# A four-layer network on one core: a sixth of the weight mixing for two batches as TensorE products, the range count moved behind layer 0, the last product with C on VectorE

## The chip, the core and the metric

The kernel runs on one core of a Trainium2 chip (trn2). A core has five engines, each with a queue of its own that is worked through in order: TensorE (PE, matrix products; its weight loads are listed apart as PEld), VectorE (DVE), ScalarE (ACT), GpSimd (POOL) and SyncE (SP), which here only issues DMAs. They meet through semaphores. Data lies in HBM, in the on-chip SBUF (128 partitions), and in PSUM, eight banks of 128 x 512 floats into which TensorE accumulates. The metric is device microseconds of one execution, as the median of several runs.

## What is computed

Three images of 256 channels, 48 x 48 points, float32, go through four layers. Each adds to x a function of its group norm (32 groups of 8 channels).

```python
x = x + _L0_conv_ref(_gn(x), ...)   # 1x1 convolution, two attention + MLP blocks, 1x1 convolution
x = x + _L1_conv_ref(_gn(x), L1_conv_routing_ws, L1_conv_weight)
x = x + _L2_conv_ref(_gn(x), L2_conv_weight, L2_conv_bias)
x = x + _L3_conv_ref(_gn(x), ...)   # selective scan (Mamba) over the 2304 points
```

Layer 1 mixes eight expert kernels into one 3x3 kernel for each image, and that is what the change bears on most:

```python
pooled = x.mean(axis=(2, 3))
routing = jax.nn.sigmoid(pooled @ routing_ws)
ws = jnp.einsum('ne,eoihw->noihw', routing, weight)
...
return jax.vmap(conv_one)(xp, ws)
```

Layer 2 is one 3x3 convolution with a bias. The core of layer 3 is, for 512 inner channels and 16 states:

```python
def step(hst, inp):
    dt_t, B_t, C_t, u_t = inp
    dA = jnp.exp(dt_t[:, :, None] * A)
    hst = hst * dA + dt_t[:, :, None] * B_t[:, None, :] * u_t[:, :, None]
    y_t = jnp.einsum('bdn,bn->bd', hst, C_t)
    return (hst, y_t)
...
y = ys.transpose(1, 0, 2) + u * D_param
y = y * jax.nn.silu(z)
out = jnp.einsum('bld,cd->blc', y, out_proj_w)
```

Layer 0's softmax is taken without subtracting a row's maximum. The kernel therefore counts whether any of its sums fell out of a safe range (the tile `flag`); if one did, the whole network is run again in an exact form.

## The kernel before

The program is written with a framework that orders each engine's instructions from the data they need and from their place in the text, and gives buffers out in turn. In three stretches the order of the text is kept on PE, DVE, ACT and POOL (`keep_order`): the attention, the end of layer 0, and the scan of layer 3. In the convolutions between them it isn't: there an instruction whose data is ready may be placed ahead. Batches are taken in the order 2, 1, 0.

**Layer 0** lasts to about 1590 us. At the end of its attention the inverse sums lie in a tile; two reductions (L835, L836) and three small operations give a count `ext` for each partition, a product with a column of ones (L841) adds the partitions up, and a copy (L842) writes `flag`. Behind it PE has the second half of the last MLP block (`hidden` L491, `add_back` L502), and ACT has, ahead of its activations, DMA issues for the last 1x1 convolution (L862, L864). Along with that convolution `mixed(2, ...)` already mixes the kernels for batch 2.

**The convolutions, layers 1 and 2.** A unit is one layer and one batch: units 0 to 2 are layer 1, units 3 to 5 layer 2. A unit has two halves (24 rows), a half has two blocks of 128 output channels, and each block is an `output`: six `products` of six PE products each (L1356, weights 128x128, 288 columns; a float32 product has two instructions in the profile), PSUM copies on ACT (`cb`, L1372), and additions on DVE (L1374 to L1386). It is a Winograd form in one direction: `input_transform` makes six images of a half on DVE (L324 to L335), and `kernel_transform` makes from the three columns of the mixed kernel six kernels, by six DVE operations for each half `ct` of the input channels (L256 to L261). A unit's products start when its transformed kernels are there.

Beside units 0 and 1 the kernels of the following batch are mixed (`beside`, `mixed`): 8 experts, 2 halves of input channels, 3 columns, which is 48 pieces of 128 x 768. Each is loaded by SP (L249) into one of six buffers `wconv`. The first expert's are scaled by ACT (L273), the other seven added by DVE, one scalar_tensor_tensor a piece (L275). After each `output` 13 steps of the mixing are written. Beside unit 2 the fixed kernel of layer 2 is loaded and transformed.

After every one of the `products`, `between` takes one step of two further chains: `next_norm`, the group norm for the next use of the batch just done (ACT gives the moments L1400, L1407; PE and DVE the rest, from L184 on, with a power on POOL, L162), and, from unit 4 on, `early_preparation` of layer 3, whose steps wait for those norms. It ends with the gate's projections (`project_z`, L1186) and their copies (`take_z`).

**Layer 3** goes through 18 chunks of 384 points, 8 steps a chunk. A step loads rows of dt (L1505), fills its tile on DVE and POOL (L1535, L1539), has ACT make the decays (L1564) and DVE scan them (L1572), multiplies the states with C on POOL (`times_c`, L1580, 128x3072), sums them on PE (`add_states`, L1597) and gates the sum on DVE (`gate`, L1604). At the very end come, in this order, the sums of the last step, its gate, and for each half `mo` of the channels `project_y` (four products with `out`, L1198, then the residual through a product with the identity, L1202) and `store` (ACT copy L1209, DMA L1210). `bank` are two PSUM banks that layer 3 uses for its small products; in units 0 to 3 they are not in use.

Of the kernel before, what the change touches and what calls it, by code (L numbers as in the profile page):

```python
# [9 lines left out]
F32 = mybir.dt.float32  # L10
I32 = mybir.dt.int32
AF = mybir.ActivationFunctionType
ALU = mybir.AluOpType
# [3 lines left out]
P = 128  # L17
# [3 lines left out]
CT = 2  # L21
# [62 lines left out]
def net(  # L84
# [112 lines left out]
    def at_once(steps):  # L197

        try:
            while True:  # L200
                next(steps)
        except StopIteration as end:
            return end.value
# [56 lines left out]
        nc.vector.tensor_tensor(u[:, 3, :, ct, :], t, g1, ALU.subtract)  # L260
        nc.vector.tensor_tensor(g1, t, g1, ALU.add)  # L261

    def mixed(b, pool):

        u = weights[b] = pool.tile([P, 6, 3, CT, 256], F32, name="u")
        for e in range(EXPERTS):
            for ct in range(CT):
                for dx in range(3):
                    wt = part_of_kernel(we[e], ct, dx)
                    re = route[b][:, e : e + 1]  # L270
                    dst = u[:, dx, :, ct, :]
                    if e == 0:
                        nc.scalar.activation(dst, wt, AF.Copy, scale=re)  # L273
                    else:
                        nc.vector.scalar_tensor_tensor(dst, wt, re, dst, ALU.mult, ALU.add)  # L275
                    yield
        for ct in range(CT):
            kernel_transform(u, ct)
            yield

    def plain(pool):
        u = weights[B] = pool.tile([P, 6, 3, CT, 256], F32, name="u")
        for ct in range(CT):
            for dx in range(3):
                nc.sync.dma_start(
                    u[:, dx, :, ct, :],
                    w2[ct * P : (ct + 1) * P, dx * 768 : (dx + 1) * 768].rearrange(
                        "p (y o) -> p y o", y=3
                    ),
                )  # L290
                yield
            kernel_transform(u, ct)
            yield
# [66 lines left out]
    with ExitStack() as l0:  # L360
# [95 lines left out]
        def one():  # L456
            return psm.tile([P, 512], F32, tag="m", name="ps_m")
# [50 lines left out]
        with ExitStack() as p2:  # L508
# [323 lines left out]
            if not exact:  # L832

                ext = small.tile([P, 2], F32, name="ext")
                nc.vector.tensor_reduce(ext[:, 0:1], sums, AX.X, ALU.max)  # L835
                nc.vector.tensor_reduce(ext[:, 1:2], sums, AX.X, ALU.min)  # L836
                nc.vector.tensor_scalar(ext[:, 0:1], ext[:, 0:1], 1.0 / SUM_MIN, None, ALU.is_gt)
                nc.vector.tensor_scalar(ext[:, 1:2], ext[:, 1:2], 1.0 / SUM_MAX, None, ALU.is_lt)
                nc.vector.tensor_tensor(ext[:, 0:1], ext[:, 0:1], ext[:, 1:2], ALU.add)
                pe = one()  # L840
                nc.tensor.matmul(pe[:1, :1], ext[:, 0:1], ones[:, 0:1], start=True, stop=True)  # L841
                nc.vector.tensor_copy(flag, pe[:1, :1])  # L842

        early.close()
        psums.close()
# [92 lines left out]
        keep_order(tc, listed, mark)  # L938
        for steps in small_steps:
            at_once(steps)  # L940

# [105 lines left out]
    def in_order(t):  # L1049

        return t.rearrange("p (j n) -> p n j", j=4)
# [141 lines left out]
            k.sz = room(k, "sz")  # L1193
        nc.scalar.copy(k.sz[:, m, :], bank[j])

    def project_y(k, mo):
        for m in range(DI):
            nc.tensor.matmul(  # L1198
                bank[mo], w("out", m * 256 + mo * P, P), k.sz[:, m, :],
                start=m == 0, stop=False,  # L1200
            )
        nc.tensor.matmul(bank[mo], ident, in_order(k.ot[:, mo, :]), start=False, stop=True)  # L1202

    def residual(k):
        k.ot = room(k, "ot")
# [140 lines left out]
    with ExitStack() as l1:  # L1346
# [40 lines left out]


        units = [(layer, b) for layer in range(2) for b in ORDER]
        beside = {0: mixed(1, upools[1]), 1: mixed(0, upools[0]), 2: plain(upools[1])}  # L1390
        halves = [(k, h) for k in range(len(units)) for h in range(2)]

        def moments(b):
# [19 lines left out]
        def next_norm(layer, b):  # L1413

            last = layer and b == ORDER[-1]
            known = None if last else moments(b)
            for _ in range(5):
                yield
            _, sc, sh = yield from group_norm_steps(b, pss, "s", known=known)
            if layer == 0:  # L1420
                norms[b] = sixth(sc, sh)
            else:
                keep = const.tile([P, 2, CT], F32, name=f"norm3{b}")
                nc.vector.tensor_copy(keep[:, 0, :], sc)
                nc.vector.tensor_copy(keep[:, 1, :], sh)
                norm3[b] = keep[:, 0, :], keep[:, 1, :]
# [53 lines left out]
    with ExitStack() as l3:  # L1480
# [95 lines left out]
        def times_c(s):  # L1576
            at, m, h = steps[s]
            cb = chunks[at].bc[1][:, 2 * h : 2 * h + 2, :].unsqueeze(2)
            hc = scn.tile([P, 2, 4, CH], F32, name="hc")
            nc.gpsimd.tensor_tensor(  # L1580
                hc, tiles[s][:, :, :, 1:], cb.broadcast_to([P, 2, 4, CH]), ALU.mult
            )
            tiles[s] = hc
# [18 lines left out]
        def gate(at, m):  # L1602
            k = chunks[at]
            nc.vector.tensor_tensor(k.sz[:, m, :], k.y_ps[:, :CH], k.sz[:, m, :], ALU.mult)  # L1604
# [10 lines left out]
        for s, (at, m, h) in enumerate(steps):  # L1615
            if m == 0 and h == 1 and at + 2 <= last:
                fetch(at + 2)
            for part in range(8):
                j = 4 * m + 2 * h + part // 4
                scan(s, part)  # L1620
                decay(8 * s + part + 3)
                if part == 4 and s + 1 < len(steps):
                    first_states(s + 1)
                if part % 4 == 1:
                    if h == 1 and part == 5 and s >= 3:
                        gate(*steps[s - 3][:2])
                    run(at, j, MID)
                if part % 4 == 3:
                    run(at, j, LATE)
                if part == 3:  # L1630
                    run(at, j, PE_)
                    if s + 1 < len(steps) and h == 0:
                        more = [(at, m + 1)] if m + 1 < DI else [(at + 1, 0)]
                        for c, n in more:
                            if c <= last:
                                rows = getattr(chunks[c], "rows", {})
                                chunks[c].rows = {**rows, n: spread(chunks[c], n)}
            if s + 1 < len(steps):
                fill(s + 1)
            last_states(s)  # L1640
            times_c(s)
            run(at, 4 * m + 2 * h + 1, PE_)
            if s >= 1:
                add_states(s - 1)

            if h == 0 and s + 2 < len(steps):
                spread_pe(chunks[steps[s + 2][0]], steps[s + 2][1])
        end = len(steps) - 1
        add_states(end)
        gate(*steps[end][:2])  # L1650
        k = chunks[last]
        residual(k)
        for mo in range(2):
            project_y(k, mo)
            store(k, mo)
        keep_order(tc, listed, mark)
    late_pools.close()
# [112 lines left out]
```

## Time and profile before

| | |
|---|---|
| median of 3 runs | 3594.66 us (3594.13 to 3596.95) |
| profiled execution | 3598.05 us, its span 3596.3 us |
| mean granted TensorE clock | 0.934 |
| PE busy | 3179.0 us (88%) |
| DVE busy | 3003.0 us (84%) |
| ACT busy | 2333.6 us (65%) |
| POOL busy | 1440.4 us (40%) |

All times in the profile are of that one execution and run from the start of its span. A row of a timeline has its start, its length, the engine, the line of the kernel, the operation, what it writes and reads, a count, and in brackets how long the engine stood idle before it and what ended that. Rows of the same kind in close succession are merged. "SPq" and "ACTq" are the issue of DMAs. A row of stretches has, for one piece of the span, the busy time of each engine. Ends of matrix products are modelled.

### The profile page before, as it was taken

The numbers are of one execution on the slowest core, as the hardware profiler recorded it, in microseconds if no ns is written. First come the engines' busy times: TensorE is split into PE (matmuls) and PEld (weight loads), VectorE is DVE, ScalarE is ACT, GpSimd is POOL, SyncE is SP. The second block draws the span as 40 slices with busy tenths as digits, with TensorE's granted clock in tenths as the row PEclk, the third lists the DMA queues.
The fourth block names the chain that finished last, engine by engine and source line by source line (L and its number), as shares of the span: only waits on it lengthen the run. The fifth ranks groups of instructions, "written<-read, shape, count | busy, mean of one in ns | idle before, by whom it ended". The sixth has DMA issues, their size and how long they took to land. (4 is left out here: it accounts for less than half of the span.)

```text
span 3596.3 us, 45582 instructions
## 1 busy us (share of the span) xinstructions
PE 3179.0 (88%) x17154; PEld 1438.0 (40%) x17154; DVE 3003.0 (84%) x3304; ACT 2333.6 (65%) x3477; POOL 1440.4 (40%) x386
## 2 busy tenths in 40 slices
PE   7999999999999999977899987888888888788875
PEld 4323232352322324546677743333333333333331
DVE  4798989959989896479965379999999999999996
ACT  2788787748877875332123447777777777777774
POOL 0000000000000000210000059999999999999998
PEclk9999999999999999988999988889999999888986
DMA  4000000000000001756402234444444444444441
GB/s 181 3 1 1 1 2 1 1 40 1 1 1 1 2 1 60 243 171 219 164 28 58 60 75 116 102 112 106 111 98 111 102 108 101 118 106 107 107 106 36
DMA packets 170648, 266.50 MB, mean 74 GB/s; under 512 B 42849, under 2 KB 137633, under 8 KB 168498
## 3 DMA queue, kind: packets, MB, share of 16 engines
q1 hardware_dynamic: 152082, 243.44, 25.2%
q10 hardware_dynamic: 18336, 20.06, 1.7%
q8 instruction: 136, 2.23, 0.3%
q14 instruction: 94, 0.77, 0.1%
HBM read 216.31 MB, written 46.89 MB: 73 GB/s over the span
## 5 line engine op out<-in xcount | busy, mean ns | idle before, releaser
L610 ACT ACTIVATE pt<-ps_s 128x1024 f32<-128x1024 f32 x972 | 939.0, 1022 | 236.9 <-PE ps_s L606 219.3
L1572 DVE TENSOR_TENSOR_SCAN hs<-ps_da,hs 128x385 f32<-128x385 f32 x1152 | 1012.8, 939 | 63.2 <-ACT ps_da L1564 45.4
L686 DVE TENSOR_TENSOR part<-part,pt 128x2048 f32<-128x2048 f32 x396 | 906.5, 2289 | 79.4 <-ACT pt L610 54.8
L1564 ACT ACTIVATE ps_da<-dtr,u 128x384 f32<-128x384 f32 x1152 | 658.0, 582 | 311.1 <-DVE hs L1572 292.6
L162 POOL TENSOR_TENSOR rstd<-ve,mhalf 128x2 f32<-128x2 f32 (+1 forms) x26 | 17.9, 691 | 1529.1 <-DVE ve L160 1529.1
L606 PE MATMUL ps_s<-q,kt 32*128 32x512 f32 (+1 forms) x4320 | 615.2, 593 | 2.3 <-DVE q L567 0.9
L619 PE MATMUL acc<-pt,vt 128*32 128x512 f32 (+1 forms) x4320 | 522.3, 562 | 8.1 <-DVE o L666 8.0
L1356 PE MATMUL ps_c<-vt,u 128*128 128x288 f32 x1728 | 430.0, 410 | 45.7 <-DVE u L261 45.7
L1580 POOL TENSOR_TENSOR hc<-hs,x 128x3072 f32<-128x3072 f32 x72 | 445.6, 6188 | 37.8 <-PE ps_g L1155 13.4
L1580 POOL TENSOR_TENSOR hc<-hs,bc 128x3072 f32<-128x3072 f32 x72 | 444.1, 6169 | 37.7 <-DVE hs L1572 14.1
L1109 PE MATMUL ps_g<-u 128*128 128x384 f32 x1152 | 389.2, 493 | 3.1 <-ACT u L1118 3.1
L1356 PEld LDWEIGHTS ps_c<-vt,u 128*128 128x128 f32 x1728 | 330.3, 192 | 140.1 <-issue 34.8
L606 PEld LDWEIGHTS ps_s<-q,kt 32*128 32x128 f32 x4320 | 220.0, 183 | 388.5 <-issue 227.1
L1109 PEld LDWEIGHTS ps_g<-u 128*128 128x128 f32 x1152 | 215.0, 190 | 174.5 <-issue 14.0
L1597 PE MATMUL ps_y<-hc,u 128*32 128x384 f32 x2304 | 246.1, 550 | 30.7 <-POOL hc L1580 27.4
L1539 POOL TENSOR_TENSOR hs<-dtur,x 128x1536 f32<-128x1536 f32 x72 | 247.9, 3443 | 17.4 <-DMA dtur<-dtud 8.8
L1539 POOL TENSOR_TENSOR hs<-dtur,bc 128x1536 f32<-128x1536 f32 x72 | 248.5, 3451 | 6.5 <-ACT ps_g L1087 2.4
L619 PEld LDWEIGHTS acc<-pt,vt 128*32 128x32 f32 x4320 | 95.7, 108 | 363.8 <-issue 328.1
L1155 PE MATMUL ps_g<-wconv,u 17*128 17x384 f32 x144 | 79.2, 684 | 97.2 <-ACT x L1176 97.2
L1372 ACT COPY cb<-ps_c 128x288 f32<-128x288 f32 x48 | 19.0, 396 | 219.1 <-PE ps_c L1356 200.7
L1067 PE MATMUL ps_g<-wconv,u 128*128 128x384 f32 x144 | 87.5, 780 | 67.0 <-ACT x L1176 66.6
L1597 PEld LDWEIGHTS ps_y<-hc,u 128*32 128x32 f32 x2304 | 64.6, 118 | 201.9 <-issue 151.0
(236 smaller groups left out, 3517.1 us busy)
## 6 DMA issues: line engine op xcount, KB each, us to landing
wconv<-in_we SPq DMA_DIRECT2D x144, 384.0 KB, 4.3
dtr<-dtd SPq DMA_DIRECT2D x288, 192.0 KB, 3.8
dtur<-dtud SPq DMA_DIRECT2D x288, 96.0 KB, 4.1
wconv<-xd SPq DMA_DIRECT2D x36, 384.0 KB, 4.4
x<-bcd SPq DMA_DIRECT2D x72, 192.0 KB, 5.8
dtd<-x SPq DMA_DIRECT2D x36, 384.0 KB, 2.4
bc<-bcd SPq DMA_DIRECT2D x72, 192.0 KB, 5.5
yc<-ycat ACTq DMA_DIRECT2D x18, 576.0 KB, 4.7
```

Of the source, the lines that this page charges most:

```text
L606: nc.tensor.matmul(s[:, j, cols], kt[r, mt * P : (mt + 1) * P], q[r, :n], start=True, stop=True,)
L610: nc.scalar.activation(p[:, h0 : h0 + 2, :], s, AF.Exp)
L619: nc.tensor.matmul(acc[h * HD : (h + 1) * HD, :n], vt[:, mt, g * P + h * HD : g * P + (h + 1) * HD], p[:, h, cols], start=mt == 0, stop=mt ...
L686: nc.vector.tensor_tensor(part, first_p if group == 1 else part, p, ALU.add)
L1067: nc.tensor.matmul(bank[to], w3v["less"][:, int(to != ct), :], k.xg[:, ct, :], start=ct == 0, stop=ct == CT - 1,)
L1109: nc.tensor.matmul(bank[m % 2], w3v["wtap"][:, tap, ct, m * P : (m + 1) * P], k.xn[:, ct, tap : tap + CH], start=tap == 0 and ct == 0, sto ...
L1356: nc.tensor.matmul(pc[:, :HN], u[:, i, dy, ct, m * P : (m + 1) * P], vt[:, i, ct, dy * TW : dy * TW + HN], start=ct == 0 and dy == 0, stop ...
L1539: nc.gpsimd.tensor_tensor(hs[:, :, 2:4, 1:], k.rows[m][1].unsqueeze(1).broadcast_to([P, 2, 2, CH]), bb, ALU.mult,)
L1564: nc.scalar.activation(slots[n % 3][:, 1 : CH + 1], chunks[at].rows[m][0][:, q, :], AF.Exp, scale=amat[:, col : col + 1],)
L1572: nc.vector.tensor_tensor_scan(b, slots[(8 * s + part) % 3][:, : CH + 1], b, 0.0, ALU.mult, ALU.add)
L1580: nc.gpsimd.tensor_tensor(hc, tiles[s][:, :, :, 1:], cb.broadcast_to([P, 2, 4, CH]), ALU.mult)
L1597: nc.tensor.matmul(k.y_ps[32 * q : 32 * q + 32, :CH], fold, hc[:, g, q, :], start=False, stop=h == 1 and g == 1,)
```

## The change

Four edits:

1. `mixed` for batches 1 and 0 (`shared`): for the second half of input channels (`ct` 1) and the third column (`dx` 2), which are 8 of the 48 pieces, the mixing is done by TensorE. For each expert ACT scales the identity by the routing weight, and two products of 384 columns accumulate in the two banks `bank`; after the last expert four ACT copies bring the sum to SBUF.
2. `next_norm` waits nine steps instead of five ahead of its first TensorE product.
3. The product and the copy that end the range count stand behind the end of layer 0.
4. In the last step of layer 3 the product with C is two DVE operations of 128x1536; and of the last chunk's projection the identity product (now first) and three of the four products with `out`, for both halves, come ahead of the sums of the last step. The load of the residual moves with them.

```diff
-    def mixed(b, pool):
+    def mixed(b, pool, shared=False):
...
-                    if e == 0:
+                    if shared and ct == CT - 1 and dx == 2:
+                        flat = wt.rearrange("p y o -> p (y o)")
+                        each = tmp.tile([P, P], F32, name="each")
+                        nc.scalar.activation(each, ident, AF.Copy, scale=re)
+                        for j in range(2):
+                            nc.tensor.matmul(
+                                bank[j], each, flat[:, j * 384 : (j + 1) * 384],
+                                start=e == 0, stop=e == EXPERTS - 1,
+                            )
+                        if e == EXPERTS - 1:
+                            for y, o, n in ((0, 0, 256), (1, 0, 128), (1, 128, 128), (2, 0, 256)):
+                                at = y * 256 + o
+                                j = at // 384
+                                nc.scalar.copy(
+                                    dst[:, y, o : o + n], bank[j][:, at - 384 * j : at - 384 * j + n]
+                                )
+                    elif e == 0:
                         nc.scalar.activation(dst, wt, AF.Copy, scale=re)
                     else:
                         nc.vector.scalar_tensor_tensor(dst, wt, re, dst, ALU.mult, ALU.add)
...
-                pe = one()
-                nc.tensor.matmul(pe[:1, :1], ext[:, 0:1], ones[:, 0:1], start=True, stop=True)
-                nc.vector.tensor_copy(flag, pe[:1, :1])
...
         for steps in small_steps:
             at_once(steps)
+        if not exact:
+            pe = one()
+            nc.tensor.matmul(pe[:1, :1], ext[:, 0:1], ones[:, 0:1], start=True, stop=True)
+            nc.vector.tensor_copy(flag, pe[:1, :1])
...
-    def project_y(k, mo):
-        for m in range(DI):
+    def project_y(k, mo, lo=0, hi=DI):
+        if lo == 0:
+            nc.tensor.matmul(bank[mo], ident, in_order(k.ot[:, mo, :]), start=True, stop=False)
+        for m in range(lo, hi):
             nc.tensor.matmul(
                 bank[mo], w("out", m * 256 + mo * P, P), k.sz[:, m, :],
-                start=m == 0, stop=False,
+                start=False, stop=m == DI - 1,
             )
-        nc.tensor.matmul(bank[mo], ident, in_order(k.ot[:, mo, :]), start=False, stop=True)
...
-        beside = {0: mixed(1, upools[1]), 1: mixed(0, upools[0]), 2: plain(upools[1])}
+        beside = {0: mixed(1, upools[1], True), 1: mixed(0, upools[0], True), 2: plain(upools[1])}
...
-            for _ in range(5):
+            for _ in range(9):
                 yield
...
+            if s == len(steps) - 1:
+                for g in range(2):
+                    nc.vector.tensor_tensor(
+                        hc[:, g], tiles[s][:, g, :, 1:],
+                        cb[:, g].broadcast_to([P, 4, CH]), ALU.mult,
+                    )
+                tiles[s] = hc
+                return
...
         end = len(steps) - 1
-        add_states(end)
-        gate(*steps[end][:2])
         k = chunks[last]
         residual(k)
         for mo in range(2):
-            project_y(k, mo)
+            project_y(k, mo, 0, DI - 1)
+        add_states(end)
+        gate(*steps[end][:2])
+        for mo in range(2):
+            project_y(k, mo, DI - 1, DI)
             store(k, mo)
```

Since `project_y` is one function for all chunks, the identity product comes first in every chunk.

## The prediction

> **What bounds the kernel now.** I read three views: busy time in equal stretches, to find where which engine is full; the timeline around each edit; the chain of waits at the end. The page's averages (PE 88%, DVE 84%) mix stages. The stretches cut at the PE's own stops in units 0 to 2 of the convolutions read (us, then busy PE, PEld, DVE, ACT, POOL, granted clock, DMA share, GB/s):
>
> ```profile
> 1592.30:1665.70 73.40, 73.26 (x296) 56.67 (x296) 72.22 (x128) 13.59 (x19) 1.55 (x4) 0.97 0.63 215
> 1665.70:1685.30 19.60, 0.58 (x2) 0.51 (x3) 19.60 (x27) 13.01 (x13) 0.69 (x3) 0.56 0.70 240
> 1685.30:1757.30 72.00, 71.92 (x290) 55.93 (x290) 71.24 (x124) 10.39 (x15) 2.10 (x4) 0.98 0.59 203
> 1757.30:1774.30 17.00, 0.58 (x2) 0.50 (x2) 17.00 (x21) 7.40 (x7) 0.69 (x3) 0.59 0.63 209
> 1774.30:2098.00 323.70, 323.15 (x1286) 242.99 (x1286) 181.84 (x392) 93.89 (x125) 7.92 (x23) 1.00 0.16 42
> ```
>
> VectorE (DVE) is full in all four first rows, so DVE sets when unit 2 starts (1774.3). TensorE stands idle for 19.6 and 17.0 us in them. From 1774.3 to 2098.0 it is the reverse: PE is full, DVE half full. A gain in units 0 and 1 thus moves the start of a stretch that PE then fills without a hole, and passes on whole. The timeline names what PE waits for:
>
> ```profile
> 1668.09 8.44 DVE L275 SCALAR_TENSOR_TENSOR u<-wconv,route,u 128x768 f32<-128x768 f32 x9
> 1685.32 22.23 PE L1356 MATMUL ps_c<-vt,u 128*128 128x288 f32 x84 [14.20 <-DVE u L261]
> 1774.34 22.11 PE L1356 MATMUL ps_c<-vt,u 128*128 128x288 f32 x84 [12.29 <-DVE u L261]
> ```
>
> The mixing (L275) and then the kernel transform (L256 to L261) must end on DVE before the next unit's first product. The end of the kernel is one chain: last product with C on POOL, PE, ACT, store.
>
> **Part 1, the mixing of batches 1 and 0.** Removed from DVE: 7 instructions a batch, 14 in all. Nine in a row take 8.44 us, so 0.94 each: 13.1 us, all on DVE's full stretch; call it 13.0. Removed from ACT: one of 0.93 us a batch. Added a batch: 8 ScalarE scalings of the 128x128 identity, a form not in the trace, between 0.20 (L1404, one column) and 0.39 us (L1372, 288 columns); I take 0.28. Four PSUM copies of 128 or 256 columns, at most 0.39 each (L1372). ACT gains about 2.7 us a unit where it is busy 13.6 of 73.4: hidden. On PE: 16 products a batch, 32 instructions, since every f32 product has two here. Those of 128x384 run 32 in 10 us at full clock around 1440 (0.3125 each): 10.0 us a batch, 20.0 us in all. No DMA is added; the same 48 weight pieces are loaded.
>
> Does PE hold that? From 1592.3 to 1774.3 are 182.0 us, of which PE is busy 73.3+0.6+71.9+0.6 = 146.4. Free: 35.6; minus 20.0 added, minus the 13.0 by which the stretch shrinks: 2.6 us left. PE and DVE come out level, so stalls of one now cost. Two are new. (a) PE's queue is in order: a product waiting for its weight piece holds all convolution products behind it, and DVE waits for those. DVE waited for such pieces only 0.4 us over 98 instructions, ACT 12.9 us over 12 (the first expert). (b) At a unit's end, last piece, ACT scaling (0.28), four PE instructions (1.25) and ACT copies (up to 1.3) stand before the transform of that half: 2.8 us, against 0.94 for the DVE instruction in its place. The other half's transform (6 x 0.87 = 5.2 us) can cover this if it goes first; in the trace the halves alternate. I charge 3 us for both together; bounds 0 and, for stalls, the rivals below. Unit 2 starts 13.0 - 3.0 = **10.0 us earlier**.
>
> **The restart.** The 84 instructions after 1774.34 take 22.1 us, against 19.5 at the steady 0.2326 (43 in 10 us): 2.6 us lost after 12 us of idleness. Taking this row as it is, the loss stays. The Trainium skill, "TensorE: Matmul & The Clock Gate", Part 1, says that the array drops to half clock only after an idle window of some 3.4 us. By my sum PE ends unit 1 about when the weights are ready, so under the rule 2.6 us more go, by the row 0. I take the rule, **-2.6**, as the trace has this loss only behind long gaps.
>
> **Part 2, the norm four products later** (range 5 to 9). What units 0 to 2 give is used three units later. On PE it moves the small L184, which twice waited for ACT's moments (4.9, 4.2 us), into a place where these are done: that is why PE can use its free time; no separate gain; POOL's power L162, which moves along, finds POOL idle. In units 4 and 5 everything behind the norms in the early preparation of layer 3 moves by four products. The trace follows program order there:
>
> ```profile
> 2084.76 1.45 PE L1186 MATMUL ps_g<-u 128*128 128x384 f32 x4
> 2086.05 11.80 PE L1356 MATMUL ps_c<-vt,u 128*128 128x288 f32 x48
> 2097.93 1.82 SPq L1505 DMA_DIRECT2D dtr<-dtd  x4
> ```
>
> 48 instructions are four products: after the change the last two gate projections (L1186, eight instructions x 0.32 = 2.6 us) come behind the last product. The first load of layer 3 goes out 0.1 us after that product, so it goes up to 2.6 us earlier. The first fill on DVE (ends 2104.6; first scan 2107.6) and the PE work before it don't. Bounds -2.6 and 0; I take **-1.5**. Nothing new queues on SP.
>
> **Part 3, the flag count.** PE waited 6.2 us for it, yet little was held:
>
> ```profile
> 1408.92 1.28 ACT L496 ACT_TABLE_LOAD   x1 [6.43 <-DMA yc<-ycat]
> 1410.21 2.00 ACT L496 ACTIVATE f<-ps_s,fb 128x384 f32<-128x384 f32 x4
> 1410.98 0.19 PE L841 MATMUL ps_m<-ones,ext 128*1 128x1 f32 x2 [6.15 <-DVE ext L839]
> 1411.10 0.50 PEld L502 LDWEIGHTS acc<-f,w0b 128*128 128x128 f32 x2
> ```
>
> L502 behind it needs ACT's first activation, done at 1410.7. The wait that takes its place ends 0.35 us earlier. The moved copy costs 0.15 on DVE, in its full stretch at worst. **-0.2**; bounds -0.4 and +0.2.
>
> **Part 4, the tail.**
>
> ```profile
> 3566.86 12.27 POOL L1580 TENSOR_TENSOR hc<-hs,bc 128x3072 f32<-128x3072 f32 x2
> 3569.13 1.80 DVE L1572 TENSOR_TENSOR_SCAN hs<-ps_da,hs 128x385 f32<-128x385 f32 x2
> 3573.08 2.79 PE L1597 MATMUL ps_y<-hc,u 128*32 128x384 f32 x16 [2.16 <-POOL hc L1580]
> 3590.35 0.48 ACT L1209 COPY wconv<-ps_g 128x384 f32<-128x384 f32 x1 [3.41 <-PE ps_g L1202]
> ```
>
> The scans end at 3570.9; POOL ends its last product at 3579.1. On DVE it is two halves of 1536, nearest L1535 (1.73, one operand in PSUM): ready at 3574.4. Against this stands "SBUF — State Buffer", section "SBUF: two separate sides": a DVE instruction with two SBUF inputs and a GpSimd one that reads SBUF exclude each other, the later waits. POOL's next-to-last runs to 3573.0, so by the rule the product is ready at 3576.5. The trace has the reverse case: POOL's L883 takes 2.14 instead of 1.80 us where it starts 0.4 us before a DVE L275 ends. I take the rule; it costs nothing, as PE is later. PE, in order: next-to-last sums to 3575.9; projection ahead, 4 identity instructions x 0.655 (L1202) and 12 x 0.32 (L1198 at full clock) = 6.5, and 0.5 while the clock rises: 3582.9; last sums at full clock 1.5: 3584.4; gate 0.6; two instructions 0.7; ACT 0.48; the second half 0.6 behind: 3586.9, where before it ended at 3590.8. The stores now follow closely, so I give back 0.2: **-3.7**. All at half clock it would be +2; -4.5 at best. The residual's load, moved up too, costs nothing: the last L1206 went out at 3465.5, 120 us early, and SP's queue has nothing behind it until the stores. In the other 17 chunks the identity product moves ahead of four products; its load (3.7 us to landing) is written three half-steps, some 13 us, ahead: 0.
>
> **Sum**: -10.0 - 2.6 - 1.5 - 0.2 - 3.7 = -18.0 us. The profiled execution took 3598.05 (span 3596.30); the median, 3594.66, lies 3.4 below. The difference carries over: **3576.7, say 3577 us**.
>
> **Rivals.** *PE becomes the bound of the mixing units.* For: only 2.6 us are left, 16 pairs of new products, each in order behind a load. At 1 us of stall a pair: 16 us, less the 2.6 left and 2.6 of restart in the first unit: 10.8 of the 13.0 are gone, the later restart gain too. -2.2 - 1.5 - 0.2 - 3.7 = -7.6: 3587. Against: DVE's 0.4 us.
> *The weight pieces hold PE (slower).* A load takes 4.3 us to landing and its buffer is one of six, freed in SP's order by DVE, which may itself wait for products behind the held pair. At half a landing, 2.15 x 16 = 34.4, less 5.2: 29.2 against 13.0: +16.2 - 5.4 = +10.8: 3605. From (13.0 + 5.2)/16 = 1.15 us a pair on the mixing loses; from 1.95 on the kernel is over 0.2% slower.
> *The mixing does nothing*, the order on DVE breaking up so that the freed time is idle: -5.4, 3589. Against: DVE had other ready work through both units.
>
> **Chances.** Forecast 0.66 (3570 to 3586), PE bound 0.16, no gain of the mixing 0.08, slower 0.10. A measurement here tells 0.2% (7.2 us) from none. Faster: 0.65 + 0.11 of PE bound and 0.01 = 0.77; same 0.12; slower 0.11. Best ends together (-13 - 2.6 - 2.6 - 0.4 - 4.5) are -23.1, 3571.6; low 3570. High 3592 takes in both middle rivals.
>
> **What would show it.** L275 14 fewer; unit 2 starting near 1764 with a gap before it under 4 us and its first 84 instructions near 20 us; no PE waits on weight pieces over 1 us; L1186's last eight behind the last product; the last ACT copy some 4 us nearer to the last scan. Wrong it is if DVE shows idle stretches in units 0 and 1, or PE waits for pieces at each expert.

## The result, and the profile after

The changed kernel takes 3581.61 us (median of 4 runs, 3580.52 to 3583.59), the kernel before 3594.39 us in the same rounds (4 runs, 3592.78 to 3596.95): a ratio of 0.9964, 95% interval 0.9947 to 0.9982. The medians differ by 12.8 us, the two profiled spans by 14.4 (3596.3 and 3581.9). The forecast was 18.0 less; 3581.6 lies in its range of 3570 to 3592. Faster it is, but two of the five terms were clearly off, and they are the matter of what follows.

Busy time in stretches, cut at the first product of units 1 and 2 (columns as in the prediction: us, busy PE, PEld, DVE, ACT, POOL, granted clock, DMA share, GB/s), changed kernel:

```profile
1590.90:1677.77 86.87, 85.01 (x333) 63.43 (x333) 82.20 (x144) 17.89 (x30) 1.53 (x4) 0.97 0.63 215
1677.77:1766.19 88.42, 83.23 (x324) 62.12 (x324) 83.65 (x139) 28.21 (x43) 2.08 (x7) 0.97 0.65 220
1766.19:2090.00 323.81, 323.68 (x1290) 244.17 (x1292) 186.51 (x404) 94.58 (x126) 7.71 (x26) 0.99 0.17 45
```

The first two rows are units 0 and 1. TensorE (PE) is no longer idle for 19.6 and 17.0 us at a unit's end; it is busy for 85.0 of 86.9 and 83.2 of 88.4 us. VectorE (DVE), which was full before (1.2 and 0.8 us idle), now is idle for 4.7 and 4.8 us of them. Both engines are at 94 to 98%: they came out level, as the prediction's sum had it. In the third row PE is full as before.

Time went as follows, before and after, from the timelines. *Unit 0 to unit 2*: 182.0 and 175.3 us, 6.7 less. *Unit 2's start to the last convolution record's start*: 323.1 and 320.6, 2.5 less. *Last scan's end to the span's end*: 25.4 and 22.1, 3.3 less. Unit 0 started 1.4 us earlier, and some 0.5 us lie in the rest. (A record is one instruction of the profile.)

The waits of DVE in units 0 and 1, for the mixing line (L294, the old L275), and those of SP's queue, first the kernel before, then the changed one (us in all, times, longest):

```profile
SPq L249 <- DVE u L275: 99.3, 72, 14.3
```

```profile
SPq L249 <- DVE u L294: 68.2, 56, 10.9
...
SPq L249 <- PE ps_g L280: 18.4, 6, 8.8
```

Before, a load of a weight piece (L249) only ever stood for DVE to free a buffer of the ring, which hurts nobody as DVE was the slow one. Now it stands six times, 18.4 us, for PE's mixing product. The group line of the mixing shows what that does:

```profile
L294 DVE SCALAR_TENSOR_TENSOR u<-wconv,route,u 128x768 f32<-128x768 f32 x112 | 108.2, 1010 | 7.0 <-DMA wconv<-in_we 7.0
```

There are 112 instructions where there were 126, the 14 fewer that were counted; and DVE idled 7.0 us for pieces, where it was 0.4. The largest such wait, in the timeline of unit 1:

```profile
1717.52 2.74 PE L280 MATMUL ps_g<-wconv,each 128*128 128x384 f32 x8
...
1720.10 17.62 PE L1377 MATMUL ps_c<-vt,u 128*128 128x288 f32 x72
...
1737.56 1.45 PE L280 MATMUL ps_g<-wconv,each 128*128 128x384 f32 x4
...
1742.51 1.56 PE L280 MATMUL ps_g<-wconv,each 128*128 128x384 f32 x4 [1.07 <-DMA wconv<-in_we]
...
1745.07 1.02 DVE L294 SCALAR_TENSOR_TENSOR u<-wconv,route,u 128x768 f32<-128x768 f32 x1 [2.72 <-DMA wconv<-in_we]
```

PE takes the pieces of two experts (8 records of L280), then 72 convolution records for 17.6 us, then the next two. A piece that lands early stays in its buffer, one of six, for as long. The second of the pair at 1742.51 had not landed, and DVE's next piece, behind it on SP's queue, came 2.72 us late.

The end of the convolutions, changed kernel, answers to the lines on L1186 before (now L1206):

```profile
2081.24 5.98 PE L1377 MATMUL ps_c<-vt,u 128*128 128x288 f32 x24
2087.05 2.75 PE L1206 MATMUL ps_g<-u 128*128 128x384 f32 x8
2087.30 1.81 SPq L1526 DMA_DIRECT2D dtr<-dtd  x4
```

The last eight gate instructions stand behind the last product, and layer 3's first load goes out 0.1 us after that product's end. The flag's place:

```profile
1409.98 2.00 ACT L515 ACTIVATE f<-ps_s,fb 128x384 f32<-128x384 f32 x4
...
1410.62 1.65 PE L521 MATMUL acc<-f,w0b 128*128 128x384 f32 x2 [6.01 <-ACT f L515]
```

PE now waits 6.01 us for ScalarE's first activation, where it had waited 6.15 for the flag. And the tail, first PE's last sums in the kernel before, which stood 3.32 us for POOL's product, then the changed kernel:

```profile
3579.19 2.45 PE L1597 MATMUL ps_y<-hc,u 128*32 128x384 f32 x16 [3.32 <-POOLq L1691]
```

```profile
3555.28 6.14 POOL L1610 TENSOR_TENSOR hc<-hs,bc 128x3072 f32<-128x3072 f32 x1
...
3559.68 5.04 DVE L1604 TENSOR_TENSOR hc<-hs,bc 128x1536 f32<-128x1536 f32 x2
3561.48 2.79 PE L1627 MATMUL ps_y<-hc,u 128*32 128x384 f32 x16 [1.73 <-POOLq L1724]
...
3569.04 2.11 PE L1220 MATMUL ps_g<-sz,u 128*128 128x384 f32 x6
3571.09 1.50 PE L1627 MATMUL ps_y<-hc,u 128*32 128x384 f32 x16
...
3574.86 0.48 ACT L1230 COPY wconv<-ps_g 128x384 f32<-128x384 f32 x1 [0.17 <-PE ps_g L1220]
```

The last product with C is ready at 3564.72; PE comes to it only at 3571.09, behind the projection ahead. The last copy ends 15.6 us behind the last scan (3559.76), before 19.9.

### The profile page after: what moved, and what is told of

Same layout as the page of the kernel before. It is cut to its first block, busy times and chain, and to the rows that moved or that the text cites. A ratio compares the mean times of both kernels' runs of the same rounds, so it can differ in the third digit from the quotient of the medians.

```text
span 3581.9 us, 45734 instructions
## 1 busy us (share of the span) xinstructions
PE 3197.7 (89%) x17218; PEld 1451.1 (41%) x17218; DVE 2995.9 (84%) x3292; ACT 2337.2 (65%) x3499; POOL 1432.3 (40%) x385
## 5 line engine op out<-in xcount | busy, mean ns | idle before, releaser
L1610 POOL TENSOR_TENSOR hc<-hs,bc 128x3072 f32<-128x3072 f32 x71 | 437.9, 6168 | 36.7 <-PE ps_g L1175 13.6
L1377 PE MATMUL ps_c<-vt,u 128*128 128x288 f32 x1728 | 432.8, 411 | 20.5 <-DVE u L261 20.5
```

The lines of the kernel that those rows point to most:

```text
L1377: nc.tensor.matmul(pc[:, :HN], u[:, i, dy, ct, m * P : (m + 1) * P], vt[:, i, ct, dy * TW : dy * TW + HN], start=ct == 0 and dy == 0, stop ...
L1610: nc.gpsimd.tensor_tensor(hc, tiles[s][:, :, :, 1:], cb.broadcast_to([P, 2, 4, CH]), ALU.mult)
```

## The experiments

Single profiles of one kernel differ in two places that have nothing to do with the edits. Unit 0's first product lay between 1585.6 and 1592.3 us in all the profiles; in the stage before it PE's waits for the load `yc` came to 2.0 us in mix_one, where unit 0 starts first, and to 6.4 in spread, where it is among the last; and layer 3, from first to last scan, took 1459.6 to 1463.3 us. So each experiment is read by the lengths of the stages between, not by its total.

| kernel | unit 0 starts | units 0+1 | DVE's piece waits | unit 2 to last record | last scan to end |
|---|---|---|---|---|---|
| before | 1592.3 | 182.0 | 0.4 | 323.1 | 25.4 |
| changed | 1590.9 | 175.3 | 7.0 | 320.6 | 22.1 |
| after_again | 1589.6 | 175.2 | 6.8 | 320.7 | 22.1 |
| undo_mix | 1587.4 | 183.6 | 1.9 | 320.2 | 22.1 |
| mix_one | 1585.6 | 180.5 | 4.2 | 320.4 | 22.0 |
| own | 1586.2 | 175.3 | 7.2 | 318.9 | 24.0 |
| spread | 1592.1 | 174.8 | 5.6 | 321.7 | 22.0 |
| spread_all | (1588.9) | 171.9 | 0.5 | 320.1 | 22.1 |
| warm | 1590.1 | 173.8 | 6.5 | 319.7 | 22.2 |
| norm5 | 1590.9 | 174.6 | 5.9 | 323.8 | 22.1 |
| tail_pool | 1587.6 | 175.4 | 6.6 | 320.2 | 22.2 |
| tail_late | 1588.8 | 174.4 | 5.9 | 320.2 | 21.0 |
| best | 1589.7 | 173.1 | 4.4 | 320.2 | 20.7 |
| best_warm | 1590.1 | 172.6 | 2.7 | 320.8 | 21.0 |

(spread_all: from when unit 0 could have started, 1.10 us after the start of its last transform instruction, the distance in the others; it started at 1591.7.)

**The mixing taken back, for both batches and for one.**

```diff
-beside = {0: mixed(1, upools[1], True), 1: mixed(0, upools[0], True), 2: plain(upools[1])}
+beside = {0: mixed(1, upools[1]), 1: mixed(0, upools[0]), 2: plain(upools[1])}        # undo_mix
+beside = {0: mixed(1, upools[1], True), 1: mixed(0, upools[0]), 2: plain(upools[1])}  # mix_one
```

> The changed kernel with the shared mixing taken back for both batches; the other three parts stay. Changed kernel: 86.87 us from unit 0's first product to unit 1's, 88.42 from unit 1's to unit 2's, together 175.3, span 3581.9. Theory (the mixing alone made these two stages shorter): together 182.0 +- 0.5 as before the change, span near 3588.6. Rival (the later norm frees part of it, since its small product no longer stops PE inside the units): together 180 or less.

> Only batch 1's mixing (beside unit 0) is shared with TensorE; batch 0's (beside unit 1) is all on VectorE as before. Theory (in unit 1 the waits for weight pieces eat the gain): unit 0 to 1 near 86.9, unit 1 to 2 near 89.0, so the span only 0.5 to 1 us over the changed kernel's, and VectorE waits for pieces in unit 1 fall from 4.1 to under 1 us. Rival (each of the two gives half, and unit 1 only looks short because work slid over the border): unit 1 to 2 near 91 to 92, span 3 us over.

undo_mix gave 93.8 and 89.7 us, 183.6 in all: 1.1 over the theory's upper end, nowhere near the rival's 180. The later norm frees nothing in these two units; all of the 6.7 to 8.3 us is the mixing's. (Of the 1.6 us by which undo_mix is longer than the kernel before, DVE's waits for pieces, 1.9 in place of 0.4, make up nearly all; why they came isn't shown.) mix_one went against its theory: unit 0 took 86.6 us, but unit 1, with all of its mixing on DVE, 93.9 and not 89.0. The rival fits (91 to 92 was even short). Read unit by unit the changed kernel seemed to gain 6.1 us in unit 0 and 0.6 in unit 1; in truth work slid over the border (DVE was busy 83.65 us in unit 1 and not the 81.8 that 88.26 less seven instructions would be). Sharing batch 0 is worth 180.5 - 175.3 = 5.2 us, sharing batch 1 the other 1.5 to 3.1. (Its span, 3581.3, is no longer than the changed kernel's only because unit 0 happened to start 5.3 us earlier.)

**A buffer of its own for half of PE's pieces; the pieces spread evenly; both.**

```diff
-wt = part_of_kernel(we[e], ct, dx)
+if shared and ct == CT - 1 and dx == 2 and e % 2 == 0:        # own
+    wt = tmp.tile([P, 3 * 256], F32, name="wpe", bufs=1)
+    nc.sync.dma_start(wt, we[e][ct * P : (ct + 1) * P, dx * 768 : (dx + 1) * 768])
+    wt = wt.rearrange("p (y o) -> p y o", y=3)
+else:
+    wt = part_of_kernel(we[e], ct, dx)
...
-add = tmp.tile([P, HN], F32, name=f"add{i}")
+add = tmp.tile([P, HN], F32, name=f"add{i}", bufs=1)          # sub{i} too
```

```diff
 def between():                                                # spread
     next(pending, None)
+    for _ in range(2):
+        next(beside.get(at_unit, iter(())), None)
...
-                for _ in range(13):
+                for _ in range(1):
                     next(beside.get(k, iter(())), None)
```

> TensorE's pieces of experts 0, 2, 4, 6 get a buffer of their own beside the six of the ring (the room comes from giving VectorE's sums and differences, which only it writes and reads, one buffer in place of two). Hold theory (a piece sits in the ring until PE comes to it through 72 convolution records, and the loads behind it on SP's queue wait): VectorE's waits for pieces fall from 7.0 to under 3 us and the two stages from 175.3 to 171 to 173. Rival (PE and VectorE, both nearly full and in order, set the length; a wait that goes comes back at the next product): waits fall, stages stay at 174.5 or more.

> The mixing's steps are issued two behind each convolution product and one behind each output, not thirteen behind each output; so PE's products with the pieces stand every 36 convolution records, not two together every 72. Ring of six as in the changed kernel. Hold theory: each piece is held half as long, waits of VectorE for pieces under 3 us, stages together 171 to 173. Rival (PE/VectorE order): 174.5 or more, as the even spread only moves the waits, or PE now waits over 3 us for pieces.

Both missed what the hold theory wanted. own's waits stayed at 7.2 us and its stages at 175.3, to a tenth those of the changed kernel. Its SP queue shows why it was no clean test:

```profile
SPq L274 <- PE ps_g L287: 19.6, 2, 10.7
...
SPq L249 <- PE ps_g L287: 4.2, 3, 2.1
```

L274 is the load into the new buffer. It stood 19.6 us for PE to use the piece before, with all other loads behind it: the hold had moved, 23.8 us in place of 18.4. spread gave 174.8 us with 5.6 of waits, within the scatter of 174.4 to 175.4 over the four profiles that have the changed kernel's convolutions (changed, after_again, tail_pool, tail_late). Alone, neither helps. Whether both together do was the next run: the even spread, and all of PE's pieces in the one buffer of their own (the condition on e left out).

> Mixing steps issued two behind each convolution product (as in the run spread), and all of TensorE's pieces in one buffer of their own, so that the six of the ring serve VectorE alone. Units 0 and 1 together took 175.3 (changed kernel), 175.3 (own) and 174.8 us (spread), VectorE's waits for pieces 7.0, 7.2 and 5.6. Hold theory: only now is the ring free of held pieces; waits under 2 us and the two units in 169 to 172. Rival (in-order PE and VectorE set it): 174.5 or more whatever the waits. Second rival (one buffer makes SP's queue wait for each piece): waits over 8 us, units over 177.

The first theory held: 0.5 us of waits, 171.9 us in the two units. In unit 1, whose start needs no such correction:

```profile
1676.50:1760.82 84.32, 81.91 (x320) 61.67 (x320) 81.35 (x136) 21.56 (x32) 2.78 (x7) 0.97 0.59 198
```

84.3 us in place of 88.4, with DVE's waits for pieces there 0.3 in place of 4.1 us. Yet the queue of SP did not stop standing for PE in this run, and PE stood ahead of unit 0:

```profile
SPq L274 <- PE ps_g L287: 31.3, 9, 12.5
...
1588.98 2.90 PE L287 MATMUL ps_g<-wpe,each 128*128 128x384 f32 x4 [3.41 <-DMA wpe<-in_we]
```

That fits a cost not of the standing queue as such, but of the ring behind it running empty: with none of PE's pieces in it, six buffers serve DVE's five pieces of an expert. Which of the two edits carries more of it can't be said, as each alone gave nothing. The price is at the other end: PE stood 13.6 us in all for pieces, 13.2 of them ahead of unit 0 for batch 1's first ones, loaded one after the other, and unit 0's first product came 2.7 us late.

Two things more differ in this run. Twelve of PE's 64 mixing records stood ahead of unit 0, and unit 0 began at full clock (granted 1.00 from 1592 to 1594 us, where the changed kernel had 0.50), so PE had more room; this run can't tell their part from that of the waits. The run best, below, has neither. And not all of the gain arrived: the waits for pieces fell by 6.5 us, the two units by 3.4, as DVE then waited more for others, such as 2.3 us in unit 0 for PE's small norm product (L184).

**The restart.** Four products of no use follow the last expert's mixing product:

```diff
 if e == EXPERTS - 1:
+    warm = pss.tile([P, 512], F32, tag="s", name="ps_warm")
+    for j in range(4):
+        nc.tensor.matmul(warm[:, :384], each, xs[0 if b else 2][:, 0, :384],
+                         start=True, stop=True)
```

> The changed kernel with four products of no use on TensorE (128x384, into a free bank) behind the last expert's mixing product of both shared batches, so that the array has work in the gap before units 1 and 2. Theory (the restart at half clock is the array's idleness alone): granted clock 1.0 through both starts, the first 72 convolution records of unit 1 in about 16.8 us in place of 19.4, the first 69 of unit 2 in about 16.1 in place of 19.1; from unit 2's start to the end some 3 us less than the changed kernel's 1815.7. Rival (the slow start is not the clock but operands or queue): records stay slow, nothing gained.

The clock did as the theory had it. The starts of units 1 and 2 in the changed kernel, as rows of the timeline:

```profile
1677.77 19.42 PE L1377 MATMUL ps_c<-vt,u 128*128 128x288 f32 x72 [0.15 <-DVE u L261]
...
1766.19 23.99 PE L1377 MATMUL ps_c<-vt,u 128*128 128x288 f32 x89 [2.85 <-DVE u L261]
```

Stretches of PE around them (us, busy PE, granted clock, DMA share, GB/s), the changed kernel and then warm:

```profile
1677.77:1682.00 4.23, 4.23 (x11) 0.60 0.50 157
...
1766.19:1771.00 4.81, 4.80 (x11) 0.55 0.33 113
```

```profile
1676.66:1682.00 5.34, 3.84 (x15) 1.00 0.30 88
...
1763.92:1770.00 6.08, 5.50 (x23) 1.00 0.63 211
```

The time followed only in part. In warm PE is busy only 3.84 of 5.34 us at unit 1's start: it runs into the transform of the second half, which DVE has yet to do, and waits 1.50 us (in unit 2 0.73). Unit 1's first 72 records end 19.5 us after its start (19.4 in the changed kernel). The 16.8 us expected were too few in any case: at full clock 72 records take 17.62 us and 48 take 11.80 (rows in this text), so one takes 5.82 / 24 = 0.2425 us and not 0.2326. By that rate the restarts of the changed kernel cost PE 19.42 - 17.62 = 1.8 us in unit 1 and 23.99 - 21.7 = 2.2 in unit 2, not 3 each. From unit 2's start to the last record 319.7 us stand against 320.2 to 320.7 of the four profiles with the changed kernel's convolutions, so 0.4 to 1.0 us less, not 3; units 0 and 1 became 0.6 to 1.6 us shorter. That is 1.0 to 2.4 of the 4.0 us; the rest lies beside work that DVE has yet to do. Even the part behind unit 2's start is not clear of scatter: four kernels ran that start at full clock (own, spread_all, warm, best_warm), and the stretch took them 318.9 to 320.8 us.

**The norm alone.**

```diff
-            for _ in range(9):
+            for _ in range(5):
```

> The changed kernel with the norm back five products into the next unit in place of nine; the rest stays. Changed kernel, two profiles: units 0 and 1 together 175.3 and 175.2 us, from unit 2's start to the last convolution record 320.6 and 320.7. Theory (the later norm is worth 2.5 us at layer 3's preparation and, now that TensorE is nearly full in units 0 and 1, also frees it there of the wait for ScalarE's moments): 323.1 and 177 or more. Rival (only the preparation of layer 3 gains): 323.1 and 175.2 +- 0.6. Second rival (the 2.5 us come from something else): 320.7.

The first rival: from unit 2 to the last record 323.8 us (3.1 more), units 0 and 1 174.6 (no worse). The lines of norm5 show the gate projections between the products again, with 48 records behind them:

```profile
2075.36 2.75 PE L1206 MATMUL ps_g<-u 128*128 128x384 f32 x8
2077.94 11.80 PE L1377 MATMUL ps_c<-vt,u 128*128 128x288 f32 x48
2089.82 1.82 SPq L1526 DMA_DIRECT2D dtr<-dtd  x4
```

**The tail, one edit at a time.**

```diff
-            if s == len(steps) - 1:                           # tail_pool
+            if s == len(steps):
```

```diff
-        for mo in range(2):                                   # tail_late
-            project_y(k, mo, 0, DI - 1)
         add_states(end)
         gate(*steps[end][:2])
         for mo in range(2):
-            project_y(k, mo, DI - 1, DI)
+            project_y(k, mo)
             store(k, mo)
```

> The changed kernel with the last product with C back on POOL; the projection stays ahead of it. From the last scan's end to the end of the span the kernel before took 25.4 us, the changed one 22.1. Theory (the two edits of the tail replace each other: POOL's product would be ready near 6.1 us after its next-to-last, 3.6 us before PE has done the projection ahead): 22.1 +- 0.4. Rival (the product's engine made the gain): about 25.

> The changed kernel with the whole last projection behind the last product again; that product stays on VectorE. Theory (the two edits replace each other: PE never waits for VectorE's product, so the order of its own work is indifferent): 22.1 +- 0.4 from the last scan's end. Rival (the projection ahead made the gain): about 25.

The theory held for tail_pool to 0.1 us (22.2) and was exceeded by tail_late (21.0). Lines of tail_pool, then of tail_late:

```profile
3549.40 12.30 POOL L1610 TENSOR_TENSOR hc<-hs,bc 128x3072 f32<-128x3072 f32 x2
...
3563.07 2.12 PE L1220 MATMUL ps_g<-sz,u 128*128 128x384 f32 x6
3565.11 1.50 PE L1627 MATMUL ps_y<-hc,u 128*32 128x384 f32 x16
```

```profile
3556.28 5.33 DVE L1604 TENSOR_TENSOR hc<-hs,bc 128x1536 f32<-128x1536 f32 x2
3558.39 4.83 PE L1627 MATMUL ps_y<-hc,u 128*32 128x384 f32 x32 [2.77 <-POOLq L1722]
```

POOL's product is ready at 3561.70, 3.4 us before PE has done the projection ahead. And with DVE's product PE goes from one sum into the next, 32 records in one row, so nothing is left that the projection could fill. What cost time before was PE's wait for the product (3.32 us), and either edit takes all of it. To the last copy tail_late needs 15.3 us, the changed kernel 15.6 and 15.8 (after_again), tail_pool 15.9; the rest of tail_late's gain lies in the stores, of which the first goes out 3.9 us before the second and not 0.65. (What lies behind the last copy scatters too: own, whose last copy ends after 15.7 us, took 24.0 to the end.)

**A better version.** best joins the even spread, the own buffer (`and (e > 2 or b == 0)` in the condition) and tail_late; best_warm adds the idle products.

> The changed kernel with the even spread of the mixing's steps, TensorE's pieces in a buffer of their own from expert 3 on for batch 1 and throughout for batch 0 (experts 0 to 2 of batch 1 stay in the ring, since in the run spread_all their loads, one after the other, held unit 0's first product 2.7 us), and the whole last projection behind the last product. Hold theory: waits of VectorE for pieces under 2 us, units 0 and 1 together 170 to 172 (175.3 in the changed kernel), tail 21 to 22; median 4 to 6 us under the changed kernel's 3581.6, so 3576 to 3578. Rival (spread_all's gain was scatter of the loads before unit 0, which moved that unit's start between 1585.6 and 1592.3 us in the profiles so far): median 3580 or more.

> As best, with the four idle products of the run warm behind the last expert's mixing product of both batches. Theory (the half-clock restarts of units 1 and 2 cost about 2 us each, of which the transform of the second half gives back one): 1 to 3 us under best. Rival (VectorE's transforms set both starts, so a faster TensorE only waits for them): equal to best within 1 us.

> The changed kernel itself, unaltered, in the same rounds as the two above, to set its median against theirs and against the kernel before, and to see in one more profile how far the start of unit 0 (1590.9 us) and the length of layer 3 (1462.9 us) move from execution to execution. Theory: units 0 and 1 together 175 +- 0.6 and from unit 2's start to the last convolution record 320 to 321, wherever unit 0 starts. Rival: these lengths scatter as much as the start does, by 3 us or more, and the readings of single profiles are worth nothing.

Medians of 5 runs: best 3577.40 us (3572.35 to 3577.51), best_warm 3577.03 (3573.72 to 3581.10), the changed kernel 3580.85 (3578.92 to 3583.11), the kernel before 3596.38 (9 runs). As ratios to before: 0.9946 (0.9933 to 0.9960), 0.9950 (0.9936 to 0.9963), 0.9962 (0.9949 to 0.9976). The intervals overlap, but each of best's five runs lies under each of the changed kernel's five. The 3.4 us between the medians fit those of the stages: 2.1 in units 0 and 1, 1.4 in the tail. In best all of PE's mixing lies inside the two units, and unit 0 starts at half clock (0.50 from 1592 to 1594 us) as in the changed kernel. DVE is busy as long there, 166.2 us (165.9 in the changed kernel), and idle 2.5 us less, 6.9 in place of 9.4, which is the 2.5 us by which its waits for pieces fell (4.4, after 7.0 and 6.8). What best gained in the two units is thus what DVE no longer waited for pieces. Two of these waits stayed, both early in unit 1, so its units took 173.1 us and not 170 to 172. best_warm is equal, as its rival said. But it is a weaker test than its text has it: best itself ran unit 1's start at full clock (1.00 from 1674.2 to 1680 us), so the idle products could help unit 2's start alone.

The changed kernel's second profile gave 175.2 and 320.7 us with unit 0 starting 1.3 us earlier: the lengths of stages repeat to 0.1 us, the total does not.

## Why the prediction was nearly right, point by point

*What bounds it.* Right. DVE was the bound of units 0 and 1, and what was gained there passed on whole through units 2 to 5.

*Part 1, the mixing: -10.0 taken, -6.7 measured.* The 14 instructions went, 13.0 us of DVE. The term that was mis-sized is the 3 us "for both together", stalls behind the pieces (a) and the unit's end (b). It measured 6.3. By the rows of the two units DVE's busy time fell from 180.1 to 165.9 us, 14.2, and its idle time rose from 1.9 to 9.4, 7.5, of which 6.6 are waits for pieces; the difference is the 6.7. The step that failed is (a). The sum had looked for the stall on the wrong engine: "a product waiting for its weight piece holds all convolution products behind it", against which the 0.4 us that DVE had waited were set. PE waited 1.1 us for pieces in all. It was the piece that waited for PE, and DVE that paid: 7.0 us of waits. Idle stretches of DVE in units 0 and 1 were named as a sign of being wrong, and they are there. (b) doesn't show: DVE has no wait for the copies in these units. The 0.4 us came from a trace in which DVE freed every buffer itself within an expert; a second, in-order consumer of the same ring was not in it, so that row could not bound it. When the waits were taken away the two units came to 171.9 us, which is 10.1 less than before. That the charge of 3 us fits what is then left is luck: by then DVE waits for things that the sum did not name. Of smaller things, the scaling of the identity took 0.40 us (0.28 taken), and PE's mixing records 0.32 each (eight end 1.29 us after four, rows above), 20.6 us in all (20.0); both hidden.

*The restart: -2.6 taken, nothing measured.* Here the sum took the rule of the Trainium skill, "TensorE: Matmul & The Clock Gate", Part 1, over the row; the row (no gain) was right. Three steps failed. The 2.6 was too large: "43 in 10 us" counts records that the edges of the window cut, so 0.2326 is too short a time for one. At 0.2425 the 84 take 20.5 us, and the row's 22.1 holds a loss of 1.6; the granted clock before the change was 0.50 for the 3.0 us behind unit 2's start, half of which is 1.5. Then, PE was to end unit 1 about when the weights were ready; in the trace PE stops at 1761.7 and starts at 1766.2, with one small norm product between, and the clock went to half. At unit 1's start the clock fell behind stops of 1.70 and 0.15 us only, so there an idle stretch well under the page's 3.4 us was enough. And only part of a gain would have passed on: warm, at full clock, was 1.0 to 2.4 us shorter over both restarts together, since DVE is late there.

*Part 2, the norm: -1.5 taken, bounds -2.6 and 0.* norm5 gives 3.1 us; between the two kernels the stage is 2.5 shorter. The restart in it would account for the difference: it costs 2.2 us now and 1.6 before. The mechanism was the one named, L1206's last eight behind the last product (2.75 us) and the load 0.1 us after it. The halving for "the PE work before it" was not needed: the first scan starts 10.03 us after the last record's start, before 10.19, so all of it arrived. That the norm has "no separate gain" in units 0 and 1 was right (undo_mix, norm5), but the reason given for it was not: L184 was to come into a place where ScalarE's moments are done. It still waits for them, 5.65 and 4.31 us in undo_mix with the later norm (4.94 and 4.21 before the change), and 1.70 and 1.27 in the changed kernel, where norm5 with the early norm has 1.79 and 1.32.

*Part 3, the flag: -0.2.* L502, now L521, starts at 1410.62 in place of 1411.10, of which 0.2 us were there before this stage. So 0.3 us in its place; whether that reaches the end can't be seen, with unit 0's start scattering by 6.7 us.

*Part 4, the tail: -3.7 taken; -4.3 to the last copy, -3.3 to the end of the span.* The working in PE's order was right, and so was the rule of the Trainium skill, "SBUF — State Buffer", "SBUF: two separate sides": DVE's two halves took 5.04 us where 2 x 1.73 was the row, and ended at 3564.72, POOL's end (3561.42) plus 3.46 being 3564.88. The first half alone took 3.37 us and the second 1.75; in all twelve profiles with this product on DVE the first half starts 1.7 to 2.2 us ahead of POOL's end and ends 1.6 us behind it. It cost nothing, as said. The 0.2 us for stores that now follow closely measured 1.0. What the text did not see is that it priced one wait by two cures.

*Rivals.* "The weight pieces hold PE" named the right buffer, queue and mechanism, and was dismissed to a tenth; it happened at 3.3 us of cost and to DVE. "PE becomes the bound" did not happen, though PE is full to 94 to 98%.

The terms as measured, -6.7, 0, -2.5, -0.3 and -3.3, make -12.8 us, and the medians say -12.8. So close a fit is luck: these are single profiles, and in the later rounds the medians differ by 15.5 us (3596.38 and 3580.85). Of the 5.2 us by which the forecast of 18.0 fell short, the mixing is 3.3, the restart 2.6 and the tail 0.4; the norm gave 1.0 back.

## What to carry to other kernels

When a second in-order engine is made to read from a ring of buffers, count how long a buffer waits for that engine's turn and not only how long its instruction takes; give its tiles their own buffer and issue its work evenly. Before pricing two edits at one wait, ask what each leaves for the other. A count of instructions in a window takes in those that its edges cut; the time of one is read from two rows of different counts. Where single runs scatter, compare lengths of stages between fixed events, over a whole unit pair rather than unit by unit, as work slides over borders.

## What was not expected of the hardware

The granted clock fell to a half at unit 1's start in the changed kernel, with PE stopped for 1.70 us, then 0.38 us of a small product, then 0.15 us. It did not fall within the stop: in slices of 1 us it is 1.00 up to 1678 us, with PE at work again since 1677.77, then 0.70 and 0.50. In four more profiles (after_again, norm5, tail_pool, tail_late) it fell at this place behind stops of 1.55 to 1.90 us. Yet in mix_one it stayed at 1.00 behind a longer stop, 2.36 us, and in own, at unit 2, behind 0.35 and 1.15 us around the same product. Lines of the changed kernel, of mix_one, and of own:

```profile
1677.23 0.38 PE L184 MATMUL ps_gm<-mv,gmat 128*128 128x2 f32 x2 [1.70 <-ACT xpad L1421]
```

```profile
1671.69 0.38 PE L184 MATMUL ps_gm<-mv,gmat 128*128 128x2 f32 x2 [2.36 <-ACT xpad L1421]
```

```profile
1760.03 0.38 PE L184 MATMUL ps_gm<-mv,gmat 128*128 128x2 f32 x2 [0.35 <-ACT xpad L1428]
1761.57 10.61 PE L1384 MATMUL ps_c<-vt,u 128*128 128x288 f32 x41 [1.15 <-DVE u L261]
```

So the length of the stop alone doesn't decide, and what else does isn't shown here.

Full clock was worth little to a start that waits for another engine: without waits unit 1's 72 records would have taken 17.6 us in warm, but they ended after 19.5 (19.4 at half clock), with 1.5 us of waiting for VectorE's transform among them.
